# The last attention of a two-layer hybrid: two batch elements' quartets as one pipeline

## The chip, the cores and the metric

The kernel runs on one core of a Trainium2 chip. Its time is device microseconds of one execution, and the number to compare is the median of several runs. A core has five engines with a queue each: TensorE (PE in the profile; PEld is its weight load), VectorE (DVE), ScalarE (ACT), GpSimd (POOL) and SyncE (SP, which here only issues DMAs). Matmuls write to PSUM, which has eight banks of 512 float32 columns.

## The reference, cut to what matters

The program is two layers, each an attention, a feed-forward, another attention and the feed-forward again, on `x` of 2 x 512 x 512 in float32. The change touches the last attention and what stands around it:

```python
# L1_attn_b: B=2, S=512, E=512, H=32 heads, D=16
qkv = layernorm(x) @ qkv_w + qkv_b
q, k, v = split(qkv, 3)                  # to heads of 16
q, k = rope(q, cos, sin), rope(k, cos, sin)
scores = einsum('bqhd,bkhd->bhqk', q, k) / sqrt(D)
scores = scores + (1.0 - tril) * -66504.0
ctx = einsum('bhqk,bkhd->bqhd', softmax(scores), v)
x = x + ctx @ out_w + out_b
# L1_ffn: 8 experts, the 2 best per token
probs = softmax(h @ W_router.T)          # h = layernorm(x)
x = x + h @ W_base.T + b_base + expert_out * 2.0
```

## The kernel before, in words

Everything is kept in on-chip memory; a batch element is four tiles of 128 tokens. `k.xT[b]` holds the normalised tokens of element b, transposed. A framework (Tile) puts the instructions of each engine into an order and adds the waits; inside `manual_schedule` the order on TensorE is the one in which the program is written.

**Heads.** The heads have 16 channels. Four heads, a quartet, lie in the four strips of 32 partitions of one tile; a seventeenth row of each strip is spare and carries the row maximum into a matmul. Eight quartets are one batch element. A matmul on one strip uses 32 of the array's 128 rows, so matmuls on different strips can run side by side.

**One element** is `prepare(b)` and then `core(b)`. `prepare` (L1769) makes q and k with `rotated` (L1747): four tiles of 128 output channels, each a chain of four matmuls of 512 columns, a bias activation on ScalarE (L1755), a shuffle and a product on VectorE (L1757, L1758), a product and a sum on GpSimd (L1759, L1760); then eight DMAs deal the rows to the strips of `q` and `kk` (L1764). Between q and k it normalises the other element's tokens (b = 0) or runs `experts.begin()` (b = 1, L1611): layer norm and router front of the four tiles of element 0 that the attention has already left. `values` (L1781) makes v: four more chains.

**`core`** (L1792) goes through eight quartets as a pipeline. For a quartet there are 16 score matmuls S (query tile qt, strip g; 128 to 512 columns, since later keys are masked), each followed on VectorE by a masked maximum over its bank (L1823); `maxima` (L1834) transposes the maxima and adds them to the queries; then 16 transposed score matmuls T (key tile kc, strip g; 512 to 128 columns, L1849), each followed by an exponential on ScalarE (L1859) and, for four strips together, the triangle's cut on GpSimd (L1863); then 16 matmuls of the values, four key tiles by four strips, adding up in one bank (L1874), a copy (L1882), four transposes and the division (`divide`, L1884). The order is written by hand: `run_ordered` (L361) interleaves S and T by a string, with the strips in the orders 0, 2, 1, 3 and 1, 3, 0, 2, eight S ahead of the first quartet, and all 16 matmuls of the values in one block at a quartet's end. PSUM banks come from `k.turn()` (L145), which goes through all eight in turn.

**After the loop** the contexts are transposed, multiplied with the output weights (`chain`, L176) and added to x. The choice of the causal form is made at run time by a flag (`CausalBound`): each element has its own `tc.If`, whose other branch has the unmasked form. After both elements and outside the branches, `experts.end()` (L1618) runs: `back` of element 0, layer norm and front of element 1, and its `back`.

**Banks.** `hold` (L153) makes one tile of all eight banks; `release` gives them back to named tags (`sc` 3, `pj` 2, `tp` 2, `av` 1). The last attention runs with the tags. `HeadRooms` (L1688) allots `q`, `kk` and `v`, and `fill` (L1706) writes their constant parts on GpSimd during the expert layer before.

```python
        for b in range(B):
            prepare(b)
            with tc.If(exact != 0) as branch:
                core(b, True)
            with branch.Else():
                core(b, False)
```

Of the kernel before, what the change touches and what calls it, by code (L numbers as in the profile page):

```python
# [39 lines left out]
P = 128  # L40
# [6 lines left out]
class Block:  # L47


    def __init__(self, ctx, tc, x, out):  # L50
        nc = self.nc = tc.nc
        self.tc = tc
        self.out = out
        pool = lambda name, bufs, **kw: ctx.enter_context(tc.tile_pool(name=name, bufs=bufs, **kw))
        self.const = pool("const", 1)
        self.w = pool("w", 2)
        self.work = pool("work", 2)
        self.small = pool("small", 6)
        self.dram = pool("dram", 1, space=bass.MemoryType.DRAM)
        self.turns = 0  # L60
        self.held = None
        self.coef = None

        self.x = [
            self.const.tile([P, D], F32, tag=f"x{t}", name=f"x{t}") for t in range(NTILES)
        ]
        self.source = x
        self.load_x(0)


        self.room = self.const.tile([P, 4 * KC * S], F32, tag="room", name="room")
        parts = self.room.rearrange("p (n c s) -> p n c s", n=4, c=KC)
        self.xT = [parts[:, b] for b in range(B)]
        self.spare = [parts[:, 2 + i] for i in range(2)]
        self.spare_turn = 0
        self.ident = self.const.tile([P, P], F32, tag="ident", name="ident")
        make_identity(nc, self.ident)
        self.mhalf = self.const.tile([P, 1], F32, tag="mhalf", name="mhalf")
        nc.gpsimd.memset(self.mhalf, -0.5)
        self.ones = self.const.tile([P, 1], F32, tag="ones", name="ones")  # L80
        nc.gpsimd.memset(self.ones, 1.0)
# [46 lines left out]
    def proj(self):  # L128
        return self.bank("pj", 2)

    def tr(self):
        return self.bank("tp", 2)

    def sc(self):
        return self.bank("sc", 3)

    def av(self):
        return self.bank("av", 1)
# [14 lines left out]
    def hold(self):  # L153


        self.holding = ExitStack()
# [6 lines left out]
    def release(self, ctx):  # L163
        self.holding.close()
        self.held = None
        self.psum = ctx.enter_context(
# [1521 lines left out]
class HeadRooms:  # L1688
# [5 lines left out]
    def __init__(self, k, a, pool):  # L1694
# [9 lines left out]
        self.nm = [one([P, NT, P], f"nm{i}") for i in range(2)]  # L1704

    def fill(self, i):  # L1706
        pool = self.k.nc.gpsimd
        pool.memset(self.q[:, i], 0.0)
# [6 lines left out]
def attn_mha(k, a, exact, rooms, experts):  # L1715
# [9 lines left out]
    with ExitStack() as ctx:  # L1725
# [8 lines left out]
        bv = k.load_row(a["h_bv"], D, "h_bv", pool=lp)  # L1734
# [3 lines left out]
        v_of = lambda kc, head: v[:, (kc * H + head) * 17 : (kc * H + head) * 17 + 32]  # L1738
# [7 lines left out]

        def rotated(b, w, bias, out, queues):  # L1747
# [3 lines left out]
            for tt in range(T):  # L1751
                ps = k.proj()
                last = k.chain(ps, [(w[:, c, bass.ts(tt, P)], k.xT[b][:, c]) for c in range(KC)])
                y = full[:, tt]
                nc.scalar.activation(y, ps, AF.Identity, bias=bias[:, tt : tt + 1], scale=1.0)  # L1755
                t2 = lp.tile([P, S], F32, tag="qm", name="t2")
                nc.vector.stream_shuffle(t2, y, swap)  # L1757
                nc.vector.tensor_tensor(t2, t2, tables["sin"], ALU.mult)  # L1758
                nc.gpsimd.tensor_tensor(y, y, tables["cos"], ALU.mult)  # L1759
                nc.gpsimd.tensor_tensor(y, y, t2, ALU.add)  # L1760
# [20 lines left out]
        def values(b):  # L1781
            for t in range(NT):
                ps = k.sc()
                k.chain(ps, [(k.xT[b][:, c, bass.ts(t, P)], wv[:, c]) for c in range(KC)])
                nc.vector.tensor_tensor(
                    v[:, t * H * 17 : (t + 1) * H * 17].rearrange("p (h d) -> p h d", d=17)[:, :, 0:16],
                    ps.rearrange("p (h d) -> p h d", d=16),
                    bv.rearrange("p (h d) -> p h d", d=16),
                    ALU.add,
                )  # L1790

        def core(b, causal):  # L1792
# [3 lines left out]
            if not causal:  # L1796


                wide = S + (NT - 1) * P
                add = lp.tile([P, wide], F32, tag="add", name="add", bufs=1)  # L1800
                addT = lp.tile([P, wide], F32, tag="addT", name="addT", bufs=1)
                for m, sign in ((add, 1), (addT, -1)):
                    nc.gpsimd.memset(m, 0.0)
                    nc.gpsimd.affine_select(
                        out=m, in_=m, compare_op=ALU.is_ge, fill=masked,
                        base=sign * (S - P), pattern=[[-sign, wide]],
                        channel_multiplier=sign,
                    )

            def score(u, qt, g):  # L1810
                kv = (qt + 1) * P if causal else S
                ps = k.turn()
                nc.tensor.matmul(  # L1813
                    ps[:, :kv],
                    q[rows[g], u, bass.ts(qt, P)],
                    kk[rows[g], u, :kv],
                    start=True,
                    stop=True,
                )
                at = 32 * g + spare  # L1820
                lo = S - (qt + 1) * P
                mask = k.mask if causal else add
                nc.vector.tensor_tensor_reduce(  # L1823
                    out=ps[:, :kv],
                    in0=ps[:, :kv],
                    in1=mask[:, lo : lo + kv],
                    op0=ALU.add,
                    op1=ALU.max,
                    scale=1.0,
                    scalar=-3e38,  # L1830
                    accum_out=nm[u % 2][:, qt, at : at + 1],
                )

            def maxima(u):  # L1834
# [3 lines left out]
                t = lp.tile([P, S], F32, tag="qm", name="qm")  # L1838
                nc.vector.tensor_tensor(t, tp, q[:, u], ALU.add)
                qm[u] = t  # L1840

            def transposed(u, kc, g):
                if (u, kc) not in probs:
                    pt = lp.tile([P, 4, S], F32, tag="pT", name="pt") if kc % 2 else k.other()
                    probs[u, kc] = [pt, 0]
                pt = probs[u, kc][0]
                lo = kc * P if causal else 0
                ps = k.turn()
                nc.tensor.matmul(  # L1849
                    ps[:, lo:],  # L1850
                    kk[rows[g], u, bass.ts(kc, P)],
                    qm[u][rows[g], lo:],
# [3 lines left out]
                if not causal:  # L1856
                    at = S - P - kc * P
                    nc.vector.tensor_tensor(ps, ps, addT[:, at : at + S], ALU.add)
                nc.scalar.activation(pt[:, g, lo:], ps[:, lo:], AF.Exp, scale=scale)  # L1859
                probs[u, kc][1] += 1  # L1860
                if causal and probs[u, kc][1] == 4:
# [6 lines left out]
            def values(u):  # L1868
                acc = k.turn()
                for kc in range(NT):  # L1870
                    pt = probs.pop((u, kc))[0]
                    lo = kc * P if causal else 0
                    for g in range(4):
                        nc.tensor.matmul(  # L1874
                            acc[rows[g], lo:],
                            v_of(kc, 4 * u + g),
                            pt[:, g, lo:],
                            start=(kc == 0),
                            stop=(kc == NT - 1),
                        )  # L1880
                raws[u] = lp.tile([P, S], F32, tag="raw", name="raw")
                nc.scalar.copy(raws[u], acc)  # L1882

            def divide(u):  # L1884
                raw = raws.pop(u)
                tp = k.turn()
                for qt in range(NT):
                    nc.tensor.transpose(tp[:, bass.ts(qt, P)], raw[:, bass.ts(qt, P)], k.ident)  # L1888
                part = tp.rearrange("p (t g e) -> p t g e", g=4, e=32)
                inv = k.sm(16, "inv_all", 2).rearrange("p (t g) -> p t g", g=4)  # L1890
                nc.vector.reciprocal(inv, part[:, :, :, spare])
                nc.vector.tensor_tensor(
                    ctxt[:, :, 64 * u : 64 * u + 64].rearrange("p t (g d) -> p t g d", g=4),
                    part[:, :, :, 0:16],
                    inv.unsqueeze(3).broadcast_to([P, NT, 4, 16]),
                    ALU.mult,
                )

            with tc.manual_schedule(engines={mybir.EngineType.PE}):
                order = "STTSTSSTSTTSTSTSTTTTS|TTSTMTSSSSSS"  # L1900
                k.run_ordered(8, 8, order, score, maxima, transposed, values, divide)
            ctxT = k.other()
            for c in range(T):
                tp = k.turn()
                for t in range(NT):
                    nc.tensor.transpose(
                        tp[:, bass.ts(t, P)], ctxt[:, t, bass.ts(c, P)], k.ident
                    )
                copy = nc.scalar.copy if c % 2 else nc.vector.tensor_copy
                copy(ctxT[:, c], tp)  # L1910
            for t in range(NT):
                ps = k.turn()
                k.chain(ps, [(ctxT[:, i, bass.ts(t, P)], wo[:, i]) for i in range(T)])
                k.add_to_x(b * NT + t, ps)

        for b in range(B):
            prepare(b)
            with tc.If(exact != 0) as branch:
                core(b, True)
            with branch.Else():  # L1920
                core(b, False)
# [3 lines left out]
def kernel(ctx: ExitStack, tc: tile.TileContext, a: dict, out: bass.AP):  # L1925
    k = Block(ctx, tc, a["x"], out)
    k.hold()
# [5 lines left out]
    k.release(ctx)  # L1933
    with k.tc.tile_pool(name="f1", bufs=2) as own:
# [5 lines left out]
        experts.end()  # L1940
# [169 lines left out]
```

## Time and profile before

| what | us |
|---|---|
| three runs | 2055.39, 2055.14, 2050.83 |
| their median | 2055.14 |
| the profiled execution | 2050.64 |
| its span in the profile | 2048.9 |
| first score of element 0 | 1729.9 |
| element 0's loop and output end near | 1835 |
| first score of element 1 near | 1898 |
| element 1's output ends near | 2003.5 |
| TensorE's mean granted clock | 0.987 |

The span begins with the first recorded instruction and ends with the last; the few microseconds around it are not in the profile. In a timeline, each line gives the start, the length, the engine, the line of the kernel, the operation, what it writes and reads by the program's names, shapes and a count; in brackets stands how long the engine was idle before, and what released it. The names `sc`, `pj`, `tp` and `av` are the PSUM tags: `av` has one bank, so two uses of it follow one another on the same bank. A float32 matmul shows as two passes, each with a weight load. In the windows, each row is a stretch from A to B in us from the span's start.

### The profile page before, as it was taken

How to read it: one execution, taken by the hardware profiler on the slowest of the kernel's cores; microseconds unless marked ns; L12 is line 12 of the kernel's file. 1: busy time of each engine (PE TensorE's matmuls, PEld its weight loads, DVE VectorE, ACT ScalarE, POOL GpSimd, SP SyncE). 2: the span in 40 equal slices, each digit the busy share in tenths (PEclk: the TensorE clock that was granted, in tenths of full speed). 3: DMA queues.
4: the chain of work that ended last, by engine and by line, in shares of the span. 5: the costliest groups of instructions: out<-in, count | busy, mean ns of one | idle time of the engine just before them, and what ended most of it. 6: DMA issues, size and time to landing. Idle time of an engine off the chain costs nothing. (4 is left out here: it accounts for less than half of the span.)

```text
span 2048.9 us, 39076 instructions
## 1 busy us (share of the span) xinstructions
PE 1974.3 (96%) x15064; PEld 1107.5 (54%) x15064; DVE 1333.1 (65%) x3510; ACT 759.0 (37%) x2094; POOL 1003.5 (49%) x1288
## 2 busy tenths in 40 slices
PE   9899989999999999999999999999999989997999
PEld 5333346666666666666665545454544544654654
DVE  8779657656665566566664586666666675845854
ACT  3776622222232223222222264454445211641451
POOL 4411046675645567666653266646555544225121
PEclk9999999999999999999999999999999999999999
DMA  3010222122221222222221321020101003002001
GB/s 136 11 42 1 73 74 85 56 78 90 95 74 51 80 76 82 77 92 79 73 86 40 115 66 47 2 76 2 62 12 43 6 6 47 2 2 36 7 2 42
DMA packets 69784, 108.85 MB, mean 53 GB/s; under 512 B 13522, under 2 KB 50386, under 8 KB 62548
## 3 DMA queue, kind: packets, MB, share of 16 engines
q1 hardware_dynamic: 68660, 103.10, 16.1%
q8 instruction: 122, 2.00, 0.4%
q10 hardware_dynamic: 640, 1.05, 0.3%
q0 software_dynamic: 288, 2.10, 0.3%
q14 instruction: 74, 0.61, 0.1%
HBM read 80.00 MB, written 4.19 MB: 41 GB/s over the span
## 5 line engine op out<-in xcount | busy, mean ns | idle before, releaser
L282 ACT ACTIVATE room<-room,nmax 128x128 f32<-128x128 f32 (+3 forms) x384 | 212.1, 554 | 481.7 <-DVE nmax L272 480.7
L261 PE MATMUL held<-kT,q 128*32 128x64 f32 (+15 forms) x4096 | 264.7, 397 | 15.2 <-DVE invs L290 12.4
L293 POOL TENSOR_SCALAR room<-room,invs 128x128 f32<-128x128 f32 (+3 forms) x384 | 198.3, 536 | 153.3 <-DVE invs L290 153.3
L176 PE MATMUL held<-w,ctxT 128*128 128x512 f32 x512 | 228.8, 595 | 0.1
L272 DVE CUSTOM_DVE_ANT_0 room<-held,mask 128x128 f32<-128x128 f32 (+3 forms) x384 | 176.0, 487 | 65.6 <-PE held L261 62.0
L261 PEld LDWEIGHTS held<-kT,q 128*32 128x32 f32 x4096 | 142.5, 110 | 106.5 <-issue 28.8
L333 PE MATMUL held<-turned,vals 32*128 32x384 f32 (+7 forms) x2784 | 192.8, 421 | 2.1 <-DMA vals<-v 2.1
L570 DVE TENSOR_REDUCE nm<-held 128x1 f32<-128x512 f32 x256 | 161.7, 683 | 32.2 <-PE held L600 26.6
L333 PEld LDWEIGHTS held<-turned,vals 32*128 32x128 f32 (+1 forms) x2784 | 153.2, 169 | 39.9 <-issue 18.9
L176 PEld LDWEIGHTS held<-w,ctxT 128*128 128x128 f32 x512 | 94.7, 190 | 115.8 <-issue 108.4
L237 DVE TENSOR_TENSOR x<-held,x 128x512 f32<-128x512 f32 x120 | 81.5, 684 | 114.9 <-PE held L176 95.0
L306 DVE STREAM_TRANSPOSE turned<-room 128x1152 f32<-128x1152 f32 x80 | 109.2, 1366 | 43.5 <-POOL room L293 40.0
L1067 POOL TENSOR_TENSOR q<-q,cosq 128x512 f32<-128x512 f32 x60 | 89.4, 1491 | 59.7 <-DVE t L1064 59.7
L176 PE MATMUL held<-fold,ctxT 128*128 128x512 f32 x256 | 117.8, 604 | 0.5 <-ACT ctxT L347 0.5
L229 POOL TENSOR_TENSOR rstd<-ve,mhalf 128x1 f32<-128x1 f32 x64 | 36.8, 579 | 160.6 <-DVE ve L227 160.6
L282 ACT ACTIVATE probs<-probs,nmax 128x128 f32<-128x128 f32 (+3 forms) x128 | 71.1, 556 | 67.3 <-DVE nmax L272 66.1
L1023 PE MATMUL held<-room,w 128*128 128x256 f32 x384 | 95.1, 384 | 0.0
L293 POOL TENSOR_SCALAR probs<-probs,invs 128x128 f32<-128x128 f32 (+3 forms) x128 | 66.0, 535 | 58.9 <-DVE invs L290 56.9
L176 PE MATMUL sc<-w,room 128*128 128x512 f32 x208 | 92.7, 592 | 0.0
L1068 POOL TENSOR_TENSOR q<-q,t 128x512 f32<-128x512 f32 x64 | 88.0, 1374 | 6.5 <-DVE q L1067 2.5
L305 DVE STREAM_TRANSPOSE turned<-room 128x128 f32<-128x128 f32 x80 | 24.3, 304 | 101.3 <-POOL room L293 101.1
L1023 PEld LDWEIGHTS held<-room,w 128*128 128x128 f32 x384 | 71.4, 190 | 32.3 <-issue 21.6
(333 smaller groups left out, 4425.0 us busy)
## 6 DMA issues: line engine op xcount, KB each, us to landing
w<-in_b_wq SPq DMA_DIRECT2D x16, 1024.0 KB, 4.8
w<-in_b_wo SPq DMA_DIRECT2D x16, 1024.0 KB, 5.0
vals<-v SPq DMA_DIRECT2D x256, 64.0 KB, 2.0
w<-in_m_wo SPq DMA_DIRECT2D x8, 1024.0 KB, 4.8
w<-in_b_wk SPq DMA_DIRECT2D x16, 256.0 KB, 2.6
w<-in_b_wupv SPq DMA_DIRECT2D x16, 256.0 KB, 2.6
w<-in_m_wqn SPq DMA_DIRECT2D x8, 384.0 KB, 3.0
x<-in_x SPq DMA_DIRECT2D x8, 256.0 KB, 4.1
```

Source lines behind the costliest of these rows:

```text
L176: last = self.nc.tensor.matmul(out, lhsT, rhs, start=(i == 0), stop=(i == len(pairs) - 1))
L237: self.latest = self.nc.vector.tensor_tensor(self.x[t], ps, self.x[t], ALU.add).ins
L261: nc.tensor.matmul(ps[32 * i : 32 * i + 32, a - lo : b - lo], q[:, at : at + 32], keys[:, a:b], start=True, stop=True,)
L272: nc.vector.tensor_tensor_reduce(out=row, in0=ps[:, :kv], in1=self.mask_back[:, :kv] if qt % 2 else self.mask[:, S - kv :], op0=ALU.add, o ...
L282: nc.scalar.activation(row, row, AF.Exp, bias=nmax, scale=-1.0, accum_out=total[:, qt : qt + 1])
L293: self.nc.gpsimd.tensor_scalar(row, row, inv[:, qt : qt + 1], 1.0, ALU.mult, ALU.mult)
L306: self.nc.vector.transpose(out[:, :last], probs[:, :last])
L333: self.nc.tensor.matmul(out[:, :, :n], values(i, j), rhs, start=(j == blocks[0]), stop=(j == stop[i]),)
L570: k.latest = nc.vector.tensor_reduce(nm[u % 2][:, qt, at : at + 1], ps, AX.X, ALU.max, negate=True).ins
L1023: nc.tensor.matmul(out, lhsT[:, c], rhs[:, c], start=c == 0, stop=c == 1)
L1067: mul.tensor_tensor(q, q, tables["cosq"], ALU.mult)
L1068: nc.gpsimd.tensor_tensor(q, q, t2, ALU.add)
```

## The change

Both elements' quartets, 16 units, become one pipeline in one branch (`causal`); the other branch keeps the form of before for both elements. `prepare(0)` stays ahead; then `k.hold()` gives the eight banks as one tile: banks 0 to 2 for S (and the maxima's transposes), 3 to 5 for T, 6 for the values, 7 for everything else (`k.ring = (7,)`).

A unit has eight steps. In each, two S go to one pair of strips and two T to the other pair. After every second step come the four value matmuls of one key tile, three key tiles behind; after the other steps `slices` issues two units of cost from `pieces`: the chains of element 1's q, k and v, the divisions, then element 0's context transposes, output chains, layer norms and router fronts. S runs twelve pairs ahead of the loop; after each of these stands one matmul of a piece.

Element 1 needs room. Its first two quartets go to four new tiles (`rooms.more`, filled by GpSimd with the others), the rest to the places of quartets of element 0 that are done; its values go to the weights of q and k, after those are used; element 0's transposed contexts go to the weights of v. The rotated tiles pass through four buffers in `k.xT[0]`, and 64 DMAs of 16 x 512 on SP deal them out, in place of twelve. `turn_pairs` takes its scratch from the pool of the layer norm's rows (`xn`, two buffers) where it had its own. `experts.begin` for element 0 is taken apart into pieces, and `experts.end()` stands inside both branches.

```diff
     def proj(self):
-        return self.bank("pj", 2)
+        return self.bank("pj", 2) if self.held is None else self.turn()
...
+        def turn_pairs(y, ps, bias):
+            nc.scalar.activation(y, ps, AF.Identity, bias=bias, scale=1.0)
+            t2 = k.work.tile([P, S], F32, tag="xn", name="t2")
+            nc.vector.stream_shuffle(t2, y, swap)
+            nc.vector.tensor_tensor(t2, t2, tables["sin"], ALU.mult)
+            nc.gpsimd.tensor_tensor(y, y, tables["cos"], ALU.mult)
+            nc.gpsimd.tensor_tensor(y, y, t2, ALU.add)
...
+            banks = {"S": (0, 1, 2), "T": (3, 4, 5)}
+
+            def own_bank(kind):
+                turns[kind] = (turns[kind] + 1) % 3
+                return k.held[:, banks[kind][turns[kind]]]
...
+            scores = iter(
+                [(n, qt, p) for n in range(16) for qt in reversed(range(NT)) for p in range(2)]
+            )
+
+            def next_scores():
+                at = next(scores, None)
+                if at:
+                    n, qt, p = at
+                    for g in (2 * p, 2 * p + 1):
+                        score(n, qt, g)
...
+            def values_of(n, kc):
+                b, u = divmod(n, 8)
+                acc = k.held[:, 6]
+                pt = probs.pop((n, kc))[0]
+                lo = kc * P
+                for g in range(4):
+                    nc.tensor.matmul(
+                        acc[rows[g], lo:],
+                        own(b, kc, 4 * u + g),
+                        pt[:, g, lo:],
+                        start=(kc == 0),
+                        stop=(kc == NT - 1),
+                    )
+                if kc == NT - 1:
+                    raws[n] = lp.tile([P, S], F32, tag="raw", name="raw")
+                    nc.scalar.copy(raws[n], acc)
+                    pieces.insert(1, (0, divided(n)))
...
+            pieces = [
+                (gate, p)
+                for tt, gate, then in ((0, 0, 0), (1, 0, 2), (2, 0, 4), (3, 2, 6))
+                for gate, p in (
+                    (gate, rotated_tile("q", tt)),
+                    (gate, rotated_tile("k", tt)),
+                    (then, store(tt)),
                 )
+            ]
+            pieces += [(2, fill_values())] + [(2, value_tile(t)) for t in range(NT)]
...
+            behind = []
             with tc.manual_schedule(engines={mybir.EngineType.PE}):
+                k.ring = (7,)
+                for n in range(12):
+                    next_scores()
+                    slices(0, 1)
+                    if n == 8:
+                        maxima(0)
+                for n in range(16):
+                    for step in range(8):
+                        next_scores()
+                        for g in (2, 3) if step % 2 == 0 else (0, 1):
+                            transposed(n, step // 2, g)
+                        if step == 6 and n < 15:
+                            maxima(n + 1)
+                        if step % 2 == 0 and len(behind) > 2:
+                            values_of(*behind.pop(0))
+                        else:
+                            slices(n, 2)
+                        if step % 2:
+                            behind.append((n, step // 2))
+                k.ring = (0, 1, 2, 3, 4, 5, 7)
+                for at in behind:
+                    values_of(*at)
+                slices(16, 1000)
...
+            experts.end()
+
+        prepare(0)
+        k.hold()
+        with tc.If(exact != 0) as branch:
+            causal()
+        with branch.Else():
+            core(0)
+            prepare(1)
+            core(1)
+            experts.end()
```

The number in a piece's pair is its gate: the unit before which it isn't issued. Once quartet 7 of element 0 is divided, `leave` adds element 0's context, output, layer norm and front to the pieces:

```python
            def leave():
                last = [begin()] + [context(0, c) for c in range(T)] + [output(0, t) for t in range(NT)]
                for t in range(NT):
                    last += [normal(t), front(t)]
                return last
```

## The prediction, made before the changed kernel was run

> **What bounds the kernel now.** I read the page first, then busy time by windows over the last attention, then two timelines of one period of its loop.
>
> On the page TensorE is the engine that is nearly always busy, at full clock in almost all slices, so the time goes where TensorE's queue goes. (A busy PE is not a PE at its peak: its matmuls are pipelined.)
>
> ```profile
> PE 1974.3 (96%) x15064; PEld 1107.5 (54%) x15064; DVE 1333.1 (65%) x3510; ACT 759.0 (37%) x2094; POOL 1003.5 (49%) x1288
> ```
>
> The windows cut the stage: start of element 0's loop, its steady part, its output, element 1's preparation, start of element 1's loop, its steady part, its output, the expert layer. Columns: length, busy us of each engine, granted clock, DMA share, GB/s.
>
> ```profile
> 1729.90:1744.00 14.10, 11.58 (x79) 8.70 (x79) 13.13 (x57) 1.95 (x4) 0.00 (x0) 0.76 0.01 3
> 1744.00:1812.00 68.00, 67.70 (x690) 40.74 (x690) 55.24 (x221) 41.30 (x116) 17.86 (x28) 1.00 0.01 2
> 1812.00:1835.00 23.00, 22.92 (x119) 12.03 (x112) 4.83 (x9) 7.44 (x20) 2.55 (x4) 1.00 0.01 3
> 1835.00:1898.00 63.00, 51.55 (x146) 26.01 (x144) 34.68 (x108) 8.50 (x16) 31.13 (x24) 0.92 0.24 34
> 1898.00:1911.00 13.00, 10.60 (x75) 8.30 (x76) 12.51 (x55) 1.50 (x3) 0.00 (x0) 0.87 0.00 1
> 1911.00:1990.00 79.00, 78.63 (x779) 47.38 (x775) 58.34 (x229) 48.57 (x135) 20.40 (x32) 1.00 0.01 1
> 1990.00:2003.50 13.50, 13.50 (x35) 6.12 (x34) 2.34 (x4) 0.74 (x2) 0.00 (x0) 1.00 0.02 5
> ```
>
> The reader should see what the change can win: the two starts (14.1 and 13.0 us, DVE full, clock 0.76 and 0.87) and the preparation, where PE is idle 11.5 us at clock 0.92. All else is PE at work.
>
> One period of the loop, PE's timeline:
>
> ```profile
> 1779.46 1.06 PE L1874 MATMUL sc<-room,vs 128*32 128x512 f32 x8
> ...
> 1781.39 0.43 PE L1874 MATMUL sc<-pt,vs 128*32 128x128 f32 x8
> 1781.75 0.58 PE L1813 MATMUL pj<-ks,qs 32*128 32x384 f32 x1
> ...
> 1789.59 1.06 PE L1874 MATMUL sc<-room,vs 128*32 128x512 f32 x8
> ```
>
> A unit (a quartet) takes 1789.59-1779.46 = 10.13 us: the values 2.29 (in one block), the two transposes 0.59 and 0.58, scores and transposed scores (S and T) 6.67.
>
> And how long a bank is bound by one T of 512 columns, in the tile "av", which has a single bank:
>
> ```profile
> 1771.63 0.69 PE L1849 MATMUL av<-qm,ks 32*128 32x512 f32 x1
> ...
> 1772.17 0.59 PE L1849 MATMUL av<-qm,ks 32*128 32x512 f32 x1
> ...
> 1772.85 0.60 ACT L1859 ACTIVATE room<-av 128x512 f32<-128x512 f32 x1 [0.51 <-PE sc L1849]
> ...
> 1773.50 0.29 PEld L1849 LDWEIGHTS av<-qm,ks 32*128 32x128 f32 x2
> ```
>
> Each float32 matmul is two passes. From first pass to the next user of the bank: 1773.50-1771.63 = 1.87 us. With eight shared banks before, few wait for that.
>
> **The change, part by part.** The sum runs from the first score (1729.9) to the end of the last output chain (2003.5): 273.6 us before. What lies ahead and behind (expert layer, 45.4 us) keeps its work.
>
> *Prices.* A matmul holds its 32-row strip for 0.54+0.43 = 0.97 us at 512 columns, 0.75 at 384, 0.53 at 256, 0.32 at 128 (same timeline, first pass to second, second to the next on the strip). Bound bank, T: 1.9, 1.6, 1.2, 0.9. Bound bank, S: 1.73 at 384 (1771.63 to 1773.36 in that timeline, with the DVE reduction of 0.57), so about 2.1 at 512 (reduction 0.73), 1.4 and 1.0. A full 128x128 matmul of 512 columns: eight passes took 1825.23 to 1828.66, 0.86 each. Four 128-column transposes: 0.43. Changing between strips, values and full matmuls leaves the array empty: values' last passes start 1781.39, stream 0.21, S begins 1781.75: 0.15; into the values 0.18, into transposes 0.10.
>
> *The new order of a unit*, read from the order in which the changed kernel's instructions stand. Eight steps, each two S on two strips and two T on the other two. Columns, S: 256 256 128 128 512 512 384 384; T: 512 512 384 384 256 256 128 128. After steps 0, 2, 4, 6 comes a quarter of the values; after 1, 3, 5, 7 a slot for up to two pieces' matmuls. S and T have three banks each. So the second S of a step waits for the reduction of the step before's first S, and the second T for its exponential; being in order, all behind it waits too.
>
> A unit without pieces, beginning with step 1. Steps 1 and 2: second T of step 2 at 1.87, 0.74 more, then 0.18 + values 0.43 + 0.15: 3.37 us. Steps 3 and 4: second S at 1.03, T at 1.57, end 2.10, values 0.21 + 0.33: 2.64. Step 5, the divide's transposes, step 6 (second S waits 2.1 after step 4's and step 5's), maxima's transposes, values 0.85: 4.53. Steps 7 and 0: the second S of step 0 waits 1.73, ends 2.69, values 0.64 + 0.33: 3.66. Sum **14.2 us against 10.13**. Of the 4.1 us some 2 are the bank waits; the rest is switches (four values blocks for one) and unequal lengths in a step.
>
> *Pieces* ride in the odd slots: a pair of matmuls (1.72) after step 1, 3, 5, 7 adds 1.06, 1.97, 1.03, 0.98 to its unit, for it fills the bank wait. All pieces use one bank. Where a piece ends and another begins in one slot, the new one waits for the evacuation, about 1.0 us (0.17 + 0.6 to 0.7 + 0.2): ten times in the listing. Each router front keeps that bank until its last DVE operation; between 1864.77 and 1868.41 in the timeline of before two such chains took 3.6 us, so I add 2 us for each of four.
>
> Units 0 to 15 then: 23.2 (seven slots but few values), 14.2, 19.8, 20.8, 19.8, 16.4, 14.2, 14.2, 16.6, 20.4, 19.8, 23.0, 22.7, 14.2, 12.4 and 9.4 (scores are used up): 281 us.
>
> *Lead*: 12 S pairs, each with one piece matmul: 4 x (0.97+0.25+0.86) + 4 x 1.86 + 2 x 1.64 + 2 x 1.43, and maxima 0.6: 22.5 us. It replaces a 14.1 us start but does three projection chains.
>
> *Tail*: last values, divide, context transposes and copies 7.6, sixteen output matmuls 13.7: 21.3 us.
>
> *Ahead of it*: the pair products' scratch now shares two buffers with the layernorm's rows, which so come after POOL's products of four tiles (3.0 us each: rows of 1.69 and 1.31): I reckon 2.6 us of PE waiting; the PSUM hold makes the first score wait for the last value tile's add (0.7) and its signal: 1.2. Bounds 0 (other work of PE covers it) and 8 (two more tiles of POOL). The four more fills on POOL cost 2.3 us (0.53 and 0.61 each) beside a DVE-bound stretch: nothing; if that cover is gone, 2.3.
>
> *Moved stores*: 64 small DMAs on SP in place of 12 from before; SP's issue took 0.6 each and landed after 4.5. ScalarE's bias activation of a later tile waits for an earlier tile's stores, and the exponentials queue behind it. The tightest is the seventh tile: its stores begin with unit 2, 8 x 0.6 + 4.5 = 9.3 us later, about when its chain ends: 0, at worst 5. SP has nothing else due then but the bias row.
>
> *Gone*: the second start, the idle time of the preparation, one branch and the four half-clock spells. All are inside the 273.6, so they need no term.
>
> Sum: 22.5 + 281 + 21.3 + 3.8 = 329 against 273.6: **+55**. The profiled execution took 2050.64 us (its span 2048.9 and 1.7 around it); plus 55 is 2106. The runs' median, 2055.14, is 4.5 above it; 2108 lies between the two bases.
>
> [...] The rows show an empty array at each change of kind, 0.10 to 0.18 us. [...] By the rows a unit had three excursions from the strips and now has up to nine, 0.3 us each: six more in 16 units are 29 of the 55 us. [...]
>
> **Rivals.**
>
> *Switches only.* The bank waits are hidden (the scheduler's evacuations come quicker than my chains). A unit is then 6.8 (the longer of S and T in each step) - 0.4 + 4 x 0.33 + 2.13 + 1.2 = 11.0; 40 slots at 1.97 less what they overlap add 66. 176 + 66 + 44 = 286: +13, 2064. For it: DVE and ScalarE have spare time. Against: the 1.87 us is latency, and spare time does not shorten it.
>
> *Faster.* One mechanism: consecutive steps overlap on the strips, so the pairs run like the old interleaving at 10.1 us a unit, while the preparation hides in the slots. 22.5 + 16 x 10.1 + 64 piece matmuls x 0.86 + 21.3 = 260: -13, 2038. For it: in the PE timeline a later matmul does start on its free strip before an earlier one on a busy strip. Against: semaphore waits stand in the one queue, and a values block follows every second step. It decides below 10.9 us a unit.
>
> *Half clock.* The loop's gaps let the clock fall, as between 1736.5 and 1743 (clock 0.50 after 2.3 us of waiting). A third of the 281 us at half clock, on about 11 of 14.2 us of streaming, adds 60 or more: 2170. Against: steady parts with sub-microsecond gaps show 1.00.
>
> That the changed branch is not taken is excluded: the score rows have 128 to 512 columns, which is the causal form, and the flag's data stay.
>
> **How the numbers follow.** Forecast (2085 to 2140) 0.60; switches only (2053 to 2085) 0.18; faster 0.13; half clock (above 2140) 0.09. The range 2053 to 2145 leaves out the faster case and most of the half clock. A measurement of this kernel tells about 0.3% (6 us) from no change. Faster by more 0.13, within 0.05 (the low edge of switches only), slower 0.82.
>
> **What would show it.** A unit without pieces (units 1, 6, 7, 13) near 14 us between values blocks; PE waiting for DVE and ScalarE at the second S and T of even steps; slots' first matmuls waiting for the bank; clock 1.00 throughout; no idle gap over 3 us before the expert layer. I am wrong if such a unit takes under 11 us.

## The result, and the profile after

Medians: 2128.75 us for the changed kernel (four runs, 2123.69 to 2141.61) and 2052.98 for the one before (four runs, 2049.13 to 2055.39): ratio 1.038, 95% interval 1.0331 to 1.043. It is slower by some 76 us. The profiled execution took 2128.38 (span 2126.7, mean clock 0.978; before 2050.64, 2048.9, 0.987). The page still shows TensorE as the busy one. The number of weight loads is the same, and they are busy for a little less time (1087.0 us, 1107.5 before):

```profile
PE 2039.4 (96%) x15064; PEld 1087.0 (51%) x15064; DVE 1336.7 (63%) x3510; ACT 767.1 (36%) x2094; POOL 1003.7 (47%) x1294
```

Windows of the changed kernel, columns as before: the lead; from unit 0's first values to unit 6's; from there to unit 7's (no pieces but a division); from unit 11's to unit 12's; the tail.

```profile
1742.35:1765.97 23.62, 23.42 (x76) 8.04 (x76) 15.93 (x54) 1.37 (x2) 5.57 (x4) 1.00 0.08 19
...
1784.86:1894.15 109.29, 103.05 (x673) 38.68 (x672) 60.92 (x224) 41.15 (x105) 25.25 (x32) 0.97 0.06 14
1894.15:1907.72 13.57, 13.03 (x106) 5.86 (x105) 8.88 (x36) 6.69 (x18) 2.54 (x4) 1.00 0.00 1
...
1986.46:2019.94 33.48, 24.74 (x141) 12.13 (x141) 19.57 (x101) 9.27 (x24) 3.83 (x5) 0.71 0.00 0
...
2062.17:2081.64 19.47, 18.76 (x79) 9.27 (x77) 8.23 (x18) 2.20 (x5) 4.82 (x6) 0.92 0.00 1
```

A unit without pieces takes 13.57 us against 10.13, at full clock; the one with three of the four router fronts takes 33.48, at clock 0.71. The second start and the idle preparation are gone, and the first start has become the lead; the whole is longer all the same.

The timelines of PE and its weight loads show that unit. It begins and ends with the first quarter of the values (L1998); S is L1941, T is L1976.

```profile
1894.15 1.06 PE L1998 MATMUL held<-room,vs 128*32 128x512 f32 x8
1895.15 0.19 PEld L1941 LDWEIGHTS held<-more 32*128 32x128 f32 x2 [0.84 <-DVE nm L1877]
...
1896.77 0.18 PEld L1941 LDWEIGHTS held<-more 32*128 32x128 f32 x1 [0.94 <-DVE nm L1877]
...
1897.83 0.16 PEld L1998 LDWEIGHTS held<-pt,vs 128*32 128x32 f32 x8 [0.76 <-POOL pt L1987]
1898.62 0.19 PEld L1941 LDWEIGHTS held<-more 32*128 32x128 f32 x2 [0.62 <-DVE nm L1877]
...
1900.44 0.29 PEld L1976 LDWEIGHTS held<-qm,ks 32*128 32x128 f32 x2 [0.24 <-ACT room L1983]
...
1907.72 1.07 PE L1998 MATMUL held<-room,vs 128*32 128x512 f32 x8
```

The weight load of a score stands and waits for the VectorE reduction (L1877) of an earlier score in its bank, and the queue behind it waits too. Over the whole run the view of the score's line says what ended the idle time before it (us, times), before and after:

```profile
  DVE nm L1823: 8.5, 19
```
```profile
  DVE nm L1877: 42.2, 64
  issue: 32.1, 70
```

For the second line ("issue", 4.6 us in 17 waits before) the profile names no releaser. T waits less for its exponentials, 9.7 us in 20 waits (11.6 in 58 before):

```profile
  ACT pt L1983: 5.1, 10
  ACT room L1983: 4.6, 10
```

**Where the 77.8 us between the two spans lie.** 4.6 lie ahead of any changed code (the expert layer's first router chain starts at 1637.83 instead of 1633.26; in the profiles of all kernels here that point lies between 1628.8 and 1638.1, so this is variation and not the change). The expert layer with its fills, up to q's first chain, takes 55.8 instead of 53.7: +2.1. From there to the first score 48.7 instead of 43.0: +5.7. From the first score to the first transpose of the expert layer at the end 339.3 instead of 273.2: +66.1. What follows takes 45.1 instead of 45.9: -0.8.

Below, "the stretch" is that one from first score to the expert layer at the end. It is free of what varies ahead of it, so the experiments are compared by it as well as by their times. Each ratio is to runs of the kernel before that were made beside the experiment.

### The profile page after: what moved, and what is told of

It is laid out like the page before. It is cut to its first block, busy times and chain, and to the rows that moved or that the text cites. A ratio compares the mean times of both kernels' runs of the same rounds, so it can differ in the third digit from the quotient of the medians.

```text
span 2126.7 us, 39092 instructions
## 1 busy us (share of the span) xinstructions
PE 2039.4 (96%) x15064; PEld 1087.0 (51%) x15064; DVE 1336.7 (63%) x3510; ACT 767.1 (36%) x2094; POOL 1003.7 (47%) x1294
## 3 DMA queue, kind: packets, MB, share of 16 engines
q1 hardware_dynamic: 69748, 103.63, 15.4%
## 4 chain that ended last, share of the span: by engine, by line
PE 87%; DVE 8%; POOL 3%; issue 1%; ACT 1%; DVEq 0%; POOLq 0%; ACTq 0%
PE held L176 24%; PE held L261 11%; PE held L333 9%; PE held L1023 9%; PE held L1941 4%; PE held L2012 3%; PE held L1976 3%; PE held L610 3%; PE held L964 3%; PE held L562 2%; PE held L1998 2%; PE held L447 2%; PE sc L176 2%; PE held L1345 2%; DVE nm L570 2%; PE held L1342 1%
## 5 line engine op out<-in xcount | busy, mean ns | idle before, releaser
L237 DVE TENSOR_TENSOR x<-held,x 128x512 f32<-128x512 f32 x136 | 92.7, 685 | 144.1 <-PE held L176 116.7
L1877 DVE CUSTOM_DVE_ANT_0 held<-held,mask 128x512 f32<-128x512 f32 (+3 forms) x256 | 121.3, 513 | 92.3 <-PE held L1941 91.6
L229 POOL TENSOR_TENSOR rstd<-ve,mhalf 128x1 f32<-128x1 f32 x64 | 36.7, 577 | 153.7 <-DVE ve L227 149.3
L1941 PE MATMUL held<-ks,qs 32*128 32x384 f32 (+3 forms) x448 | 103.9, 499 | 4.2 <-DVE nm L1877 3.1
L1976 PE MATMUL held<-qm,ks 32*128 32x384 f32 (+3 forms) x448 | 101.2, 499 | 1.8 <-ACT pt L1983 1.1
L282 ACT ACTIVATE probs<-probs,nmax 128x128 f32<-128x128 f32 (+3 forms) x128 | 71.1, 556 | 67.2 <-DVE nmax L272 66.1
```

The costliest lines, as they stand in the source:

```text
L282: nc.scalar.activation(row, row, AF.Exp, bias=nmax, scale=-1.0, accum_out=total[:, qt : qt + 1])
L1877: nc.vector.tensor_tensor_reduce(out=ps, in0=ps, in1=mask, op0=ALU.add, op1=ALU.max, scale=1.0, scalar=-3e38, accum_out=nm[u % 2][:, qt, a ...
L1941: nc.tensor.matmul(ps, held(b, u, q_of)[rows[g], bass.ts(qt, P)], held(b, u, k_of)[rows[g], :kv], start=True, stop=True,)
L1976: nc.tensor.matmul(ps[:, lo:], held(b, u, k_of)[rows[g], bass.ts(kc, P)], qm[n][rows[g], lo:], start=True, stop=True,)
```

## The experiments

Theory **banks**: three banks for S and three for T make the in-order queue wait for evacuations. Rival **switches**: the four quarter blocks of values, each an excursion from the strips, cost the time. Third, **fronts**: the layer norms and router fronts among the pieces, and the half clock.

**1. Values in one block.**

```diff
-                        if step % 2 == 0 and len(behind) > 2:
-                            values_of(*behind.pop(0))
-                        else:
+                        if step == 0:
+                            while behind:
+                                values_of(*behind.pop(0))
+                        elif step % 2:
                             slices(n, 2)
```

> The changed kernel with a unit's four values blocks issued together, behind the next unit's first pair of transposed scores, instead of a quarter after every second step; nothing else moves. Theory 'switches' (the excursions from the strips cost 0.3 us each): three excursions fewer, an unsliced unit goes from 13.57 to about 12.6 us and the whole from 2128 to about 2112. Theory 'banks' (the second S and second T of a step wait for the evacuation of a bank three matmuls back): the quarters stood where PE waits for a bank anyway, so taking them away gives most of the wait back; unit 13.0 to 13.6, whole 2119 to 2128.

Measured 2158.56 us, ratio to before 1.0518 (1.0488 to 1.0547); a unit without pieces 14.24 us. So neither: it is 30 us slower than the changed kernel. The edit also takes three slots from unit 0 (steps 0, 2 and 4), so that its pieces move to later units; a unit without pieces isn't touched by that. Here part of the next unit's exponentials overwrote probabilities before the values read them, so a second form put the block between the step's S and T:

```diff
                         next_scores()
+                        if step == 0:
+                            while behind:
+                                values_of(*behind.pop(0))
                         for g in (2, 3) if step % 2 == 0 else (0, 1):
```

> The changed kernel with a unit's four values blocks issued together between the next unit's first pair of scores and its first pair of transposed scores (in values_once the next unit's first pair of exponentials overwrote two of the four probability blocks before the values read them, and the values waited for them; here the order is sound). Theory 'switches': three excursions of 0.3 us fewer, an unsliced unit goes from 13.57 to about 12.6. Theory 'banks': the quarters filled bank waits, so the unit stays at 13.2 to 13.9.

Measured 2178.71 us (two runs; ratio 1.0614, 1.058 to 1.0648), the unit 14.37:

```profile
1915.10 1.07 PE L1998 MATMUL held<-room,vs 128*32 128x512 f32 x8
...
1929.47 1.07 PE L1998 MATMUL held<-room,vs 128*32 128x512 f32 x8
```

and VectorE in the same unit (timeline), waiting for the first score behind the block:

```profile
1918.98 0.43 DVE L1877 CUSTOM_DVE_ANT_0 held<-held,mask 128x256 f32<-128x256 f32 x1 [3.28 <-PE held L1941]
```

With three excursions fewer the unit is 0.8 us longer. VectorE stands still for 3.28 us, while the block of 2.29 us and the first scores behind it run; that its reductions then come in a crowd, and that a quarter gives it time to catch up, is the likely reading and isn't shown by itself. What "switches" expected, 12.6 us for one block instead of four, is refuted; what an excursion costs by itself isn't separated from the wait. The units with pieces grew by more (25 to 26 us where the changed kernel had 19 to 22, with windows at clock 0.74 to 0.93): they hold the pieces moved out of unit 0 too, and the rest isn't taken apart.

**2. Number of banks.** In the changed kernel, S gets bank 7 and the pieces take theirs from this ring (an open chain's bank is skipped):

```diff
-            banks = {"S": (0, 1, 2), "T": (3, 4, 5)}
+            banks = {"S": (0, 1, 2, 7), "T": (3, 4, 5)}
...
-                k.ring = (7,)
+                k.turn = lambda: own_bank("S")
```

> The changed kernel with bank 7 put into the scores' ring (four banks for S, three for T), and the pieces taking their bank from that ring; a chain that is spread over slots keeps its bank out of the ring until it is evacuated. Theory 'banks': the score matmuls' waiting for VectorE (42 us in the trace of the changed kernel) falls under 20, an unsliced unit goes from 13.57 to 12.3 to 12.9, the pieces' waits for their one bank go too, the whole to about 2105 to 2115. Theory 'switches': an unsliced unit stays within 13.3 to 13.8; only the sliced units gain, under 1 us each; whole 2118 to 2128.

Measured 2116.75 us (1.0312, 1.028 to 1.0344); the stretch 332.5, 6.8 less; the unit 13.29; waits for VectorE before S 32.3 us. The direction is that of "banks", the size is not: it asked for 12.3 to 12.9 us and under 20 us of waits, and 13.29 lies nearer to what "switches" expected. One more bank for S gives 0.28 us a unit. The views of the score's line and of T's line show where the rest went:

```profile
  DVE nm L1877: 32.3, 51
```
```profile
  ACT room L1995: 9.9, 16
  ACT pt L1995: 9.1, 16
```

S waits 9.9 us less for VectorE, and T, still with three banks, waits 19.0 us for ScalarE where it waited 9.7: most of the wait moved from one ring to the other. The stretch with the fronts stayed long (39.98 us), so bank 7 alone was not what held it.

In the kernel before, six banks in place of eight:

```diff
-    BANKS = (
-        ("sc", 3), ("pj", 2), ("tp", 2), ("sc", 3), ("pj", 2), ("tp", 2), ("sc", 3), ("av", 1)
-    )
+    BANKS = (("sc", 3), ("pj", 2), ("sc", 3), ("av", 1), ("sc", 3), ("pj", 2))
...
-            self.turns = (self.turns + 1) % 8
+            self.turns = (self.turns + 1) % 6
```

> The kernel before with its old order, but the last attention's scores, transposed scores, maxima, values and divides turning over six banks in place of eight. Theory 'banks': the number of banks alone lengthens the old period of 10.13 us, to 11 to 12 us; sixteen units make the whole 14 to 30 us slower than before, 2067 to 2083. Theory 'switches': the old order has one values block and the same strips, so the period stays within 10.1 to 10.4 and the whole within 5 us of before.

Measured 2086.39 us (1.0168, 1.0137 to 1.0199). Its periods, from values to values:

```profile
1749.43 1.07 PE L1872 MATMUL av<-room,vs 128*32 128x512 f32 x8
...
1761.18 1.07 PE L1872 MATMUL sc<-room,vs 128*32 128x512 f32 x8
```

11.75 us instead of 10.13: two banks fewer alone cost 1.62 us a unit. "Banks" holds for the old order. The whole lost some 35 us, more than the 14 to 30 expected: the fourteen periods between values blocks are 19.5 us longer together, and from element 0's last values to element 1's first it took 111.4 us instead of 99.3.

**3. Equal lengths.** Sixteen pairs of scores ahead in place of twelve, so that S and T of a step have the same columns:

```diff
-                for n in range(12):
+                for n in range(16):
```

> The changed kernel with sixteen pairs of scores ahead of the loop in place of twelve, so that in each step S and T have the same number of columns (512 with 512, 128 with 128); banks, switches and pieces stay. If the unequal lengths in a step are part of the 3.4 us that a unit has over the old order (a step lasts as long as its longer kind: 6.9 us of strips a unit now, 5.1 with equal lengths, at 0.97/0.75/0.53/0.32), an unsliced unit falls by 0.9 to 1.7 us, to 11.9 to 12.7, and the whole by 12 to 25 us. If the waits for banks alone set the steps, the strips' time is covered and the unit stays within 0.4 of 13.57.

Measured 2115.28 us (1.0289, 1.025 to 1.0328); the stretch 326.9, 12.4 less; the unit:

```profile
1888.42 1.07 PE L1998 MATMUL held<-room,vs 128*32 128x512 f32 x8
...
1900.84 1.07 PE L1998 MATMUL held<-room,vs 128*32 128x512 f32 x8
```

12.42 us: unequal lengths were 1.15 of the unit's excess of 3.44 over the old order (13.57 against 10.13).

**4. The fronts behind the loop.**

```diff
-                for t in range(NT):
-                    last += [normal(t), front(t)]
                 return last
...
+                pieces.extend((0, p) for p in route())
                 slices(16, 1000)
```

(`route` holds the pieces taken out of `leave`.)

> The changed kernel with the four layernorms and router fronts of element 0 issued behind the loop instead of in its slots. If they are what made the stretch from unit 11's to unit 12's values 33.5 us (half clock in it), that stretch falls to 20 or less, and with some 4 to 7 us for them behind the loop the whole is 6 to 12 us faster than the changed kernel, about 2118. If the stretch was long for another reason (the unit's own S and T at half clock), it stays over 25 us and the whole within 4 us of 2128 or above it.

Measured 2116.70 us (1.0323, 1.03 to 1.0347); the stretch 321.8, 17.5 less. The period that was 33.48 is 13.57. Over the last seven periods the loop lost 24.2 us, and the part behind it, from the last unit's values on, grew from 22.1 to 31.2. In the timeline of the changed kernel one sees how a front in a slot costs that: the piece behind it, the next tile's transposes (L214), waits for the end of the routing chain on VectorE (L1568).

```profile
1990.76 0.28 DVE L1568 TENSOR_TENSOR hw<-held,comb 128x128 f32<-128x128 f32 x1
1991.09 0.71 PEld L214 LDWEIGHTS held<-ident,xn 128*128 128x128 f32 x4 [3.32 <-DVE hw L1568]
...
2006.26 0.29 DVE L1568 TENSOR_TENSOR hw<-held,comb 128x128 f32<-128x128 f32 x1
2006.61 0.42 PEld L214 LDWEIGHTS held<-ident,xn 128*128 128x128 f32 x4 [2.57 <-DVE hw L1568]
```

The clock was at half for 6.8 us from within the first of these waits (1990.2) and for 13.65 us from just behind the second (2007.25).

**5. Scratch of its own for element 0's preparation.**

```diff
-            t2 = k.work.tile([P, S], F32, tag="xn", name="t2")
+            t2 = pool.tile([P, S], F32, tag=tag, name="t2")
...
-                turn_pairs(full[:, tt], ps, bias[:, tt : tt + 1])
+                turn_pairs(full[:, tt], ps, bias[:, tt : tt + 1], lp, "qm")
```

> The changed kernel with the pair products' scratch of element 0's preparation in buffers of its own, as before the change; the pieces keep the shared ones. The stretch from q's first chain to the first score took 48.7 us against 43.0 before. If the shared buffers are the cause (rows of the layernorm wait for GpSimd's products), it falls by 2 to 4 us and the whole by as much, to about 2125; if the PSUM hold or the clock is, it stays over 47.5 us.

Measured 2116.39 us (1.0315, 1.0294 to 1.0336). From q's first chain (1685.96) to the first score (1730.07) 44.1 us instead of 48.7: 4.6 are the shared buffers' (more than the 2 to 4 expected), with the half clock behind their wait: in the changed kernel a gap of 2.9 us near 1713 with 3.4 us at half clock behind it, of which this run has neither. 1.1 over the 43.0 of before are left for the hold. The rest of the 12 us between the medians is mostly not its doing: in its profile the unchanged stages ahead ended 7.2 us earlier.

**6. All four mends of the pairs.**

> The changed kernel's pairs with all four mends together: sixteen pairs ahead (lead16), four banks for scores (score_ring4), scratch apart (own_scratch), layernorms and fronts behind the loop (fronts_after). If the parts add up: unsliced unit 12.42 less 0.3, 12.1; whole 2128.75 less 13.5, 12, 12.4 and 12, about 2080. If banks are what is left of the unit's excess over 10.13, the fourth bank gives more now that the steps are shorter: unit 11.6 or less, whole 2070. In both cases it stays behind the kernel before, for quarter blocks and pairs remain.

Measured 2081.38 us (1.0148, 1.0122 to 1.0175); the unit 12.00:

```profile
1858.07 1.06 PE L2010 MATMUL held<-room,vs 128*32 128x512 f32 x8
...
1870.07 1.06 PE L2010 MATMUL held<-room,vs 128*32 128x512 f32 x8
```

The stretch is 302.6, 36.7 less than the changed kernel's, and 17.5 + 12.4 + 6.8 = 36.7: the parts add up. The fourth bank now gives 0.42 a unit, more than the 0.28 it gave alone, but "banks" had named a unit of 11.6 or less. A unit still has 1.87 us over the old order; the page of this run has 4.1 us of idle time ahead of T's matmuls (without that of their weight loads), 2.2 of them until an exponential.

**7. The old order in one branch.** `run_ordered` over sixteen units with all eight banks in turn, values in one block, pieces as whole chains behind it. The heart of the edit:

```diff
+                order = "STTSTSSTSTTSTSTSTTTTS|TTSTMTSSSSSS"
+                k.run_ordered(16, 8, order, score_ahead, maxima, transposed, values, after)
```

> One branch and one pipeline of sixteen units as in the changed kernel, with element 1's preparation and element 0's output and routing as pieces between, but in the old order of single strips with one values block a unit on eight shared banks; the pieces are whole chains behind a unit's values (seven of them, six projection chains and a group of stores, between the first scores), the scratch as in own_scratch. Theory 'banks' (with 'switches' behind it): the merging itself is good, and what lost was the order with three banks a kind: an unsliced unit is back at 10.1 to 10.4, the loop with its pieces some 255 us against 273.6 before, the whole 2030 to 2042, faster than both. If merging itself costs (pieces in the loop, their VectorE work, the clock), units with pieces are over 16 us and the whole is above 2050.

Measured 2061.46 us (1.0051, 1.0029 to 1.0073). The unit without pieces is back at 10.19:

```profile
1770.05 1.06 PE L1981 MATMUL held<-room,vs 128*32 128x512 f32 x8
...
1780.24 1.07 PE L1981 MATMUL held<-room,vs 128*32 128x512 f32 x8
```

But the stretch is 283.1: not 255, and 10 over before. The whole is above 2050 and several units with pieces take over 16 us, which is what the rival, "merging itself costs", named. The periods with fronts took up to 23.2 us. The timeline has the same wait, now of T behind a front:

```profile
1924.76 1.19 PE L1958 MATMUL held<-qm,ks 32*128 32x512 f32 x1 [3.92 <-DVE hw L1568]
```

So the fronts' layer norms and routers go to the last output chains, where VectorE has little to do (the lead's chains also move, behind every third score, and element 0's output chains each one unit later):

```diff
+                normal(1)
+                for c in range(T):
+                    context(1, c)
+                for t, more in enumerate(((front, 0), (normal, 2, front, 1), (normal, 3, front, 2, front, 3), ())):
+                    for f, at in zip(more[::2], more[1::2]):
+                        f(at)
+                    output(1, t)
```

> old_order with element 0's layernorms and router fronts taken out of the loop and put between the last four output chains, and with the six projection chains between the first scores after every third score rather than every second. In old_order the four periods with fronts took 2.4, 9.3, 8.7, 0.7 and 3.3 us more than a unit with an output chain or none, with idle TensorE of 2.8 to 3.9 us for VectorE's routing chain and half clock behind it. If that is where the merging's gain went: the loop 24 to 28 us shorter, the end 5 to 7 longer, the lead 4 to 6 shorter; the whole 2033 to 2042, faster than both kernels. If the fronts cost as much wherever they stand, the whole stays at 2052 or above.

Measured 2044.64 us, ratio 0.9962 (0.9945 to 0.998): faster than both kernels, than the one before by 0.4%; the stretch 267.7, 15.4 less. So most of what cost was the fronts' place, and not the merging. The whole is 2.6 us above the range expected, and the lead did not get shorter. Two periods, 18.14 and 18.73, were still long, and the timeline suggests the cause, an early row of the layer norm on VectorE:

```profile
1897.83 0.69 DVE L191 BATCH_NORM_STATS2 ln_stats<-x 128x6 f32<-128x512 f32 x1
...
1899.59 0.55 DVE L201 TENSOR_SCALAR xn<-x,ln_mv,rstd 128x512 f32<-128x512 f32 x1 [0.67 <-POOL rstd L229]
...
1900.72 0.69 PE L1934 MATMUL held<-ks,qs 32*128 32x512 f32 x1 [1.05 <-DVE nm L1877]
```

The program has that layer norm far later; the framework's order for VectorE drew it forward. A bound on it:

```diff
-                k.layernorm(t, bias=experts.added)
+                with tc.issue_after(divided[0]):
+                    k.layernorm(t, bias=experts.added)
```

> old_order_tail with the layernorms' VectorE operations held behind the last divide that stands ahead of them. In old_order_tail two units with an output chain took 18.1 and 18.7 us where the two next took 14.8: VectorE did the row's statistics and the row (2.0 us and 0.67 us of waiting for GpSimd) right behind the output's addition, ahead of the reductions that TensorE waited for (1.05 us), and a half-clock spell followed. If that early row is the cause, both units fall to 14 to 15, the two spells go, and the whole is 5 to 8 us less than 2044.6, 2037 to 2040. If the output's addition itself delays the reductions, they stay at 17 or more and the whole is unchanged within 3 us.

Measured 2041.31 us, ratio 0.9933 (0.9918 to 0.9948). Its periods with an output chain, one after the other:

```profile
1895.14 1.06 PE L1983 MATMUL held<-room,w 128*32 128x512 f32 x8
1908.94 1.06 PE L1983 MATMUL held<-room,w 128*32 128x512 f32 x8
1922.74 1.06 PE L1983 MATMUL held<-room,w 128*32 128x512 f32 x8
```

13.80 each, and the stretch is 261.1, 12 less than before: the early row was the cause. The whole came out just above the 2037 to 2040 expected.

## Why the prediction was right, and where its terms were off

The measured 2128.75 lies within the 2085 to 2140 of the forecast and 21 us above its sum of 2108.

**The unit: mechanism and size right.** 13.57 against 14.2. The waits stand where the sum put them: the second S of step 0 starts 1.62 us after the score at 1895.15 (forecast 1.73), the second T of step 2 comes 1.82 us after the score at 1898.62 (forecast 1.87). From the score behind one values block to that behind the next, the sub-terms 3.66, 3.37, 2.64, 4.53 measured 3.47 (1895.15 to 1898.62), 3.22, 2.49 and 4.39. The splitting of its excess is less sure: more of the waiting is S's behind VectorE (42.2 us) than T's behind ScalarE (9.7). Of 3.44, unequal lengths are 1.15 and S's missing bank 0.28 to 0.42; the 1.87 that were left with both mended stay open between T's three banks, the values' own bank and the pairs. That T's waits doubled when S got its fourth bank (9.7 to 19.0 us) speaks for T's ring. A fourth bank for T wasn't tried: there is none left. The order as a whole is shown: pairs_all and old_order_tail both have the fronts out of the loop and the scratch apart, and their stretches are 302.6 and 267.7.

**Excursions: the price failed.** At the price it read from the rows, the prediction put 29 of the 55 us down to excursions. The runs with one block, which have three excursions a unit fewer, became slower, with units of 14.24 and 14.37 us against 13.57. The gaps at a change, 0.10 to 0.18 us, are the author's estimate from where the rows start; that here they partly cover waiting that would come anyway fits the slower runs and isn't shown by itself. As time that one block would win back, the price failed.

**Fronts: the mis-sized term.** "I add 2 us for each of four". With their layer norms the four cost 24.2 us in the loop, and 9.1 where they were moved behind it. A front is a chain of 16 operations on VectorE, and what stands behind it in the queue waits for its end: between the values of units 10 and 12 (1964.80 to 2019.94), TensorE is idle for 11.4 us, 6.8 of them until a front's last operation (L1568), and the clock is 0.82. The units together took 296.2 us (1765.97 to 2062.17) where 281 was forecast. By periods from values to values, units 5 to 10 together took 102.3 us where 101.6 was forecast, units 11 and 12 took 55.1 in place of 45.7, units 1 to 4 together 3 more and 13 to 15 together 3.6 more.

**Clock.** "Clock 1.00 throughout" was wrong: 0.94 over the stretch, with gaps of 1.3 to 2.7 us at four of its five slow spells. The half-clock rival had the event, at a part of its size: 41 us at half clock, not a third of the 281.

**Smaller terms.** Lead 22.5, measured 23.6; tail 21.3, measured 19.5. Ahead 3.8, measured 5.7: the hold as forecast (1.1 against 1.2), the shared buffers 4.6 in place of 2.6. Fills at 0: the expert layer was 1.6 to 2.2 us longer in the profiles of the kernels with the added fills, so they were not covered. Stores at 0: right, the bias activations (L1754) show no DMA among what they waited for. No gap over 3 us before the expert layer: right.

**Rivals.** "Switches only" and "Faster" are excluded for this kernel by the unit: 13.57, where they needed 10.9 or about 11. But "Faster", 260 us for the stretch at 10.1 a unit, is close to what old_order_late reaches with 261.1, in total and not part by part, for its pieces are whole chains: the merging itself pays, once the order of before and its eight banks are kept and the VectorE-bound pieces stand outside the loop. The profiled execution came out 22 us above the 2106 worked out for it: 15 are the units, 2.5 the smaller terms together, 4.6 what varied ahead of the change.

## What to carry to other kernels

Before splitting PSUM into rings by kind, work out how long one use binds a bank and how many matmuls lie between two uses; here rings of three left S waiting 42.2 us for VectorE where eight shared banks left 8.5, and a fourth bank for one ring moved the wait to the other. Before putting work "between" the steps of a TensorE loop, look whether the engine that evacuates the loop's banks has room for it too; here a chain of small operations on that engine was cheaper where the loop isn't (9.1 us behind it, 24.2 in it). And look in the trace for work that the framework has drawn ahead of its place.

## What the runs showed of the hardware

In the changed kernel's stretch the clock halved in five spells, of 3.4 to 13.65 us, four of them at gaps of 1.3 to 2.7 us. At the gap from 1814.92 to 1816.35 in the changed kernel (columns as in the windows above; the clock is third from the end):

```profile
1815.00:1816.00 1.00, 0.00 (x0) 0.00 (x0) 0.96 (x6) 0.07 (x1) 1.00 (x2) 1.00 0.00 0
1816.00:1817.00 1.00, 0.65 (x1) 0.50 (x2) 0.30 (x1) 0.00 (x0) 0.41 (x1) 0.55 0.00 0
...
1822.00:1823.00 1.00, 1.00 (x12) 0.16 (x8) 0.00 (x0) 0.00 (x0) 0.00 (x0) 0.53 0.15 33
1823.00:1824.00 1.00, 1.00 (x9) 0.46 (x10) 0.18 (x1) 0.10 (x1) 0.00 (x0) 1.00 0.26 60
```

At a resolution of 0.2 us the spell runs from 1816.1 to 1822.9, 6.8 us. Four more lie in the stretch: from 1921.9 to 1925.3 (3.4 us), from 1990.2 to 1997.0 (6.8), from 2007.25 to 2020.9 (13.65) and from 2055.0 to 2065.3 (10.2). From start to start it is 105.8, 68.3, 17.05 and 47.8 us; the longer spells are about two, three and four times the shortest. By estimate, from the length and a clock of 0.50, a spell of 6.8 us cost some 3.4 us where TensorE is busy throughout.

Four of the five begin in or just behind a gap of 1.3 to 2.7 us. Ahead of the last no gap was over 0.7 us. The rows at the start of the second and of the last:

```profile
1921.08 0.66 PE L1905 MATMUL held<-ident,ctx 128*128 128x128 f32 x4 [1.33 <-DVE ctx L1895]
...
2054.96 1.17 PE L1976 MATMUL held<-qm,ks 32*128 32x256 f32 x2 [0.57 <-ACT pt L1983]
```

A gap of 0.9 us near 1983, one of 1.09 ahead of the first score (1742.35), and gaps of 1.2 near 1865 and 1.1 near 1932 were followed by none. So the length of one gap doesn't decide it, and what does isn't settled here.
